# Layer 2's queries, keys, values and output projection by seven block products on the attention side

## The chip, the core and the metric

The kernel runs on one core of a Trainium2 chip. The metric is device time in microseconds (us) of that core, from launch to end; lower is better. The engines named below are PE (TensorE, matrix products), DVE (VectorE), ACT (ScalarE), POOL (GpSimd) and SP (SyncE, which here only issues DMA transfers). PEld is the loading of stationary operands into PE, and PEclk the clock that PE was granted, in parts of full speed.

## The reference

Four batches of 512 tokens by 512 features, in fp32, go through four layers. The layer that the change touches is layer 2, first half:

```
...
def _ln(x): ...                       # mean 0, variance 1 over features, eps 1e-6
qkv = (xin @ Wqkv.T + qkv_bias).reshape(Bs, Lx, 3, H, D)      # H = 16 heads of D = 32
sm  = exp(minimum(scale_mul_log, log(100)))
qn  = q / maximum(norm(q, axis=-1), 1e-12) * sm
kn  = k / maximum(norm(k, axis=-1), 1e-12)
p   = softmax(einsum('bhqd,bhkd->bhqk', qn, kn) + attn_bias)
o   = einsum('bhqk,bhkd->bhqd', p, v)  ->  (Bs, Lx, Cx)
attn = o @ Wproj.T + bproj
...
x = x + attn(_ln(x) * (scale1 + 1.0) + shift1) * gamma1
x = x + (gelu(( _ln(x) * (scale2 + 1.0) + shift2) @ Wfc1.T + bfc1) @ Wfc2.T + bfc2) * gamma2
```

Layer 0 is an attention with a sparse mask, layer 1 a full attention followed by a gated MLP, and layer 3 eight small experts with a 512 by 512 output. Layer 2 therefore has four products of 512x512 weights with 512x512 activations per batch ahead of its MLP: queries (`q2`), keys (`k2`), values (`v2`) and output (`proj2`).

## The kernel before

**Stages and streams.** Each batch passes through the stages `a01` (layers 0 and 1, attention), `m1` (layer 1's MLP), `a2` (layer 2's attention) and `m2` (layer 2's MLP, then the experts). Two streams of stages share the one core: stream A, the attention side, runs `a01`(1), `a2`(0), `a01`(2), `a2`(1), `a01`(3), `a2`(2), `a2`(3), and at the end the last batch's MLP `mlp2` and half of its experts; stream M, the other side, runs `a01`(0), `m1`(0), `m1`(1), `m2`(0), `m1`(2), `m2`(1), `m1`(3), `m2`(2) and the other half. `a2`(b) needs `m1`(b), and `m2`(b) needs `a2`(b).

**Who sets the order.** The kernel is written as generators that yield between products. A planner (`Clocks`, `interleave`) keeps an estimate of when every tile is written, how long each engine is held, and when each bank of PSUM is free; it lets the stream that is ready and furthest behind (by `WORK`, a length for each stage) take its next step. The planned start times then fix the order of instructions on each engine. On the chip an engine takes its own instructions in that order, each one waiting for its operands. In the planner, POOL's instructions and DVE's two-input ones between SBUF tiles also reserve a common `PORT` (`needs`). Side work (`chores`), such as forming sums of weights, runs in the same planner.

**Products.** `by_token` is the plain form: for each of four groups of 128 tokens, four products of 128x128 with 512 columns are summed in one PSUM bank. In `a2` all four projections had this form: 16 products of 512 columns each. `seven` is Strassen's scheme in the variant with few sums: weights and activations are cut into quarters of 256x256, the quarters and three sums on either side make seven block products, and each block product is four products of 128x128 with 256 columns, so 28 of 256 columns instead of 16 of 512. A `seven` works through parts 0 to 6; between them, part 0's result is copied out to a tile `u`, part 1's is added to it, part 3's goes with it into a tile `t`, and `take` receives the four quarters of the result, three of them with a tile still to be added:

```
x = yield from part(0);  u = side.u();  out(u, x)
y = yield from part(1);  free(y);       plus(u, y, u)
yield from part(2, x);   free(x);       take(0, 0, x, None)
y = yield from part(3);  t = side.t2(); plus(t, y, u)
x = yield from part(4);                 take(1, 1, x, t)
yield from part(5, y);   free(y);       take(0, 1, y, u)
yield from part(6, x);   free(x);       take(1, 0, x, u)
```

Before the change only side M used it, in `m1` and `mlp2_by_sevens`. The sums of activations are formed by `sums` on DVE or POOL (`add` takes the engine that the planner expects to end sooner).

**Weights.** Side M's weights come as a row of blocks (`Blocks`, tag `wm`, six tiles of two 128x512 blocks): four quarters and four sums, in the order of use; the sums are formed once by the chore `formed`, kept in DRAM, and reloaded for later batches. Side A had whole units (`Ring`, tag `wa`, two tiles of 128x4x512), loaded by one transfer of 1 MB each.

**Normalization.** After each group of 128 tokens of `q2` or `k2`, ACT squares the result (`t`), DVE sums each head's 32 squares (`ss`), POOL raises it to the power -0.5 (`inv`), for the queries DVE multiplies by `mul`, and DVE scales `t`; PE then transposes it (`heads_T`, tile `t`, L492) one product later. For `proj2`, the bias is added, POOL multiplies by the gate and adds into `x`.

In the profile, matrix products carry the line L486 and transposes L492; all DVE, ACT and POOL work carries L433, DMA loads L499.

## Time and profile before

| | |
|---|---|
| median of three runs | 2351.36 us (2350.81 to 2352.14) |
| the profiled execution's own time | 2346.66 us |
| its span, first to last instruction | 2344.9 us |
| mean granted PE clock | 0.995 |
| PE busy | 2284.7 us (97%) |
| DVE busy | 1423.9 us (61%) |
| ACT busy | 909.8 us (39%) |
| POOL busy | 876.6 us (37%) |
| DMA moved | 216.38 MB, queue of SP 28.6% of 16 engines |

An fp32 product appears in the records as two PE instructions, so a group that says x384 holds 192 products. Busy time of a group is time in which an instruction of it was the one in work; the mean of one also holds the tail in which the next is already running. The place of `a2`'s projections in the span can be read from the tile names: `q2`, `k2` and `v2` from 530 to 589 us for batch 0, 1045 to 1141 for batch 1, 1612 to 1706 for batch 2 and 1940 to 2000 for batch 3.

### The profile page before, as it was taken

How to read it: one execution, taken by the hardware profiler on the slowest of the kernel's cores; microseconds unless marked ns; L12 is line 12 of the kernel's file. 1: busy time of each engine (PE TensorE's matmuls, PEld its weight loads, DVE VectorE, ACT ScalarE, POOL GpSimd, SP SyncE). 2: the span in 40 equal slices, each digit the busy share in tenths (PEclk: the TensorE clock that was granted, in tenths of full speed). 3: DMA queues.
4: the chain of work that ended last, by engine and by line, in shares of the span. 5: the costliest groups of instructions: out<-in, count | busy, mean ns of one | idle time of the engine just before them, and what ended most of it. 6: DMA issues, size and time to landing. Idle time of an engine off the chain costs nothing.

```text
span 2344.9 us, 38165 instructions
## 1 busy us (share of the span) xinstructions
PE 2284.7 (97%) x14280; PEld 1582.9 (68%) x14280; DVE 1423.9 (61%) x3299; ACT 909.8 (39%) x2208; POOL 876.6 (37%) x1021
## 2 busy tenths in 40 slices
PE   8999999999999999999999999999999999999998
PEld 5655667885777777764677677775577786776444
DVE  5666676674675566756576465564576564785233
ACT  3665441012552452524454154243255313661313
POOL 5643321223343433433343352342334344454121
PEclk9999999999999999999999999999999999999999
DMA  3111223552224223231423323222322343223120
GB/s 117 37 60 55 83 89 115 182 184 81 73 73 122 68 100 121 77 113 36 133 80 95 117 82 104 90 77 77 99 78 86 109 148 97 75 73 126 51 82 25
DMA packets 137671, 216.38 MB, mean 92 GB/s; under 512 B 9792, under 2 KB 73312, under 8 KB 137488
## 3 DMA queue, kind: packets, MB, share of 16 engines
q1 hardware_dynamic: 136880, 213.72, 28.6%
q8 instruction: 114, 1.87, 0.3%
q14 instruction: 69, 0.57, 0.1%
q0 software_dynamic: 176, 0.15, 0.1%
q10 hardware_dynamic: 432, 0.07, 0.0%
HBM read 188.72 MB, written 25.18 MB: 91 GB/s over the span
## 4 chain that ended last, share of the span: by engine, by line
PE 54%; DVE 2%; ACT 1%; issue 1%; DMA 0%; POOL 0%; POOLq 0%; ACTq 0%; DVEq 0%
PE bank L486 39%; PE two L486 9%; PE bank L492 6%; ACT probs L433 1%; DVE mx L433 0%; PE two L492 0%; DVE probs L433 0%; DMA x<-in_x 0%; DVE hx L433 0%; DVE mt L433 0%; ACT pT L433 0%; ACT t L433 0%; DVE pT L433 0%; DVE t L433 0%; DMA arow<-in_rows 0%
## 5 line engine op out<-in xcount | busy, mean ns | idle before, releaser
L433 POOL TENSOR_SCALAR probs<-probs,inv 128x512 f32<-128x512 f32 (+4 forms) x544 | 328.1, 620 | 539.9 <-DVE inv L433 483.7
L433 ACT ACTIVATE probs<-probs,neg 128x512 f32<-128x512 f32 (+2 forms) x448 | 265.9, 595 | 188.1 <-DVE neg L433 182.9
L492 PEld LDWEIGHTS bank<-ident,probs 128*128 128x128 f32 (+1 forms) x1744 | 202.1, 141 | 82.3 <-issue 40.0
L492 PE MATMUL bank<-ident,probs 128*128 128x128 f32 (+1 forms) x1744 | 243.7, 275 | 5.1 <-ACT pT L433 3.7
L433 DVE CUSTOM_DVE_ANT_0 probs<-two,late 128x512 f32<-128x512 f32 x256 | 166.9, 685 | 34.8 <-PE two L486 23.7
L433 ACT COPY pT<-bank 128x512 f32<-128x512 f32 (+3 forms) x289 | 152.2, 547 | 68.2 <-PE bank L492 54.8
L486 PE MATMUL two<-kT,nq 32*128 32x512 f32 (+5 forms) x1088 | 149.1, 529 | 2.3 <-DVE neg L433 1.5
L433 POOL TENSOR_TENSOR inv<-ss,neg_half 128x16 f32<-128x16 f32 x32 | 92.9, 2902 | 124.4 <-DVE ss L433 124.4
L486 PE MATMUL bank<-wa_q,h 128*128 128x512 f32 x288 | 135.5, 594 | 0.3 <-ACT nq L433 0.3
L486 PE MATMUL bank<-pT,v 128*32 128x128 f32 (+2 forms) x3488 | 132.1, 275 | 3.4 <-DVE pT L433 2.1
L486 PEld LDWEIGHTS bank<-pT,v 128*32 128x32 f32 (+2 forms) x3488 | 113.2, 116 | 30.8 <-issue 17.3
L486 PE MATMUL bank<-mT,wm_gate 128*128 128x256 f32 x504 | 124.6, 382 | 3.3 <-DVE mp L433 1.5
L433 DVE COPY pT<-bank 128x512 f32<-128x512 f32 (+3 forms) x186 | 116.4, 635 | 7.2 <-PE bank L492 6.8
L433 POOL TENSOR_TENSOR x<-x,mt 128x512 f32<-128x512 f32 x60 | 80.3, 1342 | 100.4 <-DVE mt L433 100.4
L486 PEld LDWEIGHTS bank<-mT,wm_gate 128*128 128x128 f32 x504 | 92.7, 190 | 34.7 <-issue 17.5
L433 ACT COPY mu<-bank 128x512 f32<-128x512 f32 x41 | 23.9, 583 | 212.0 <-POOL x L433 108.1
L433 DVE TENSOR_REDUCE mx<-two 128x2 f32<-128x1024 f32 x64 | 77.8, 1216 | 45.2 <-PE two L486 45.1
L486 PE MATMUL bank<-wm_down,hid 128*128 128x256 f32 x408 | 101.5, 383 | 1.5 <-ACT mu L433 1.4
L433 DVE TENSOR_TENSOR x<-x,bank 128x512 f32<-128x512 f32 x93 | 63.4, 682 | 58.5 <-PE bank L486 57.9
L433 DVE RECIPROCAL inv<-total 128x2 f32<-128x2 f32 (+1 forms) x256 | 43.1, 168 | 89.5 <-ACT probs L433 76.5
L486 PE MATMUL bank<-wa_o,h 128*128 128x512 f32 x192 | 91.5, 594 | 0.0
L486 PE MATMUL bank<-mT,wm_up 128*128 128x256 f32 x360 | 89.3, 380 | 0.8 <-ACT mu L433 0.8
(389 smaller groups left out, 4694.9 us busy)
## 6 DMA issues: line engine op xcount, KB each, us to landing
wm_fc<-in_units SPq DMA_DIRECT2D x80, 256.0 KB, 2.9
wm_gate<-in_units SPq DMA_DIRECT2D x60, 256.0 KB, 3.0
wm_down<-in_units SPq DMA_DIRECT2D x52, 256.0 KB, 3.1
wm_up<-in_units SPq DMA_DIRECT2D x44, 256.0 KB, 3.0
wa_q<-in_units SPq DMA_DIRECT2D x10, 1024.0 KB, 5.2
wm_fc<-kept SPq DMA_DIRECT2D x32, 256.0 KB, 2.7
wm_fc<-kept SPq DMA_DIRECT2D x16, 512.0 KB, 3.3
wa_fc<-in_units SPq DMA_DIRECT2D x8, 1024.0 KB, 5.2
```

Source lines behind the costliest of these rows:

```text
L433: return call(*map(real, args), **{k: real(x) for k, x in kw.items()})
L486: latest[0] = nc.tensor.matmul(real(out), lhsT=real(lhsT), rhs=real(rhs), **kw)
L492: latest[0] = nc.tensor.transpose(real(out), real(src), unit)
```

## The change

`a2`'s four projections use `seven` on side A. The ring of side A becomes a row of blocks too (four tiles of two blocks, the same bytes), with a release for each block or unit; stages that take whole units take four blocks. The sums of `q2`'s and `k2`'s weights are formed by a new chore after 150 us of planned time, in tiles of side M that are free then, those of `v2` and `proj2` after `a01`(1) ends, in `pT` tiles; all are kept in DRAM and loaded from there by every batch. Activations are laid out in blocks, with `sums` for `hT` and `ctxT`. The normalization works on quarters (256 tokens by 256 features, as one 128x512 tile), in four tiles that rotate, and the transposes may lag by up to three quarters (`turns`). `proj2`'s bias times gate is added to `x` by a chore (`lift_x`) during the attention, and the result goes through `gated`. In the planner, POOL's power no longer reserves `PORT`, `scorable` and the experts' wait look at both double banks, and `a2`'s length becomes 120.8.

```diff
-WORK = {"a01": 157.8, "a2": 126.7, ...
+WORK = {"a01": 157.8, "a2": 120.8, ...
+LATER = 1.5
-WM = 6
+WM, WA = 6, 4
...
-    def needs(self, engine, op, outs, ins):
+    def needs(self, engine, op, outs, ins, func=None):
...
-        return (engine, "PORT") if wide and self.fast(outs + ins) else (engine,)
+        return (engine, "PORT") if wide and func != "pow" and self.fast(outs + ins) else (engine,)
...
-    ringA = Ring(load, clocks.tile, work, a["units"], "wa", 2, units_of(STREAM_A, ("a01", "a2", "mlp2", "half1")))
+    ringA = blocks("wa", WA, units_of(STREAM_A, ("a01", "a2", "mlp2", "half1")), A2_UNITS, False)
...
+    def formed_apart(names, staged):
+        for name in names:
+            a11, a12, a21, a22 = staged()
+            for x, which in ((a21, (1, 0)), (a22, (1, 1)), (a11, (0, 0)), (a12, (0, 1))):
+                load(quarters(x), ringA.source(name, which))
+            yield Until(lambda: clocks.written(a11, a12, a21, a22) + LATER)
+            add(a22, a21, a22, ALU.add)
+            add(a21, a11, a21, ALU.subtract)
+            add(a11, a22, a11, ALU.subtract)
+            add(a12, a12, a11, ALU.subtract)
...
+                    sync.dma_start(out=kept[:, j - at.start, :], in_=x)
+            ringA.formed.add(name)
+
+    def formed_for_a2():
+        yield Until(150.0)
+        yield from formed_apart(A2_UNITS[:2], lambda: [*sideM.sums(), sideM.u()])
+        yield When(lambda: ("a01", 1) in ended)
+        yield from formed_apart(A2_UNITS[2:], lambda: halved(sideA.pT(2)))
...
         def scorable():
-            return max(locked[0], clocks.free("two", 2, 2))
+            return max(locked[0], clocks.free("two", 2), clocks.free("two", 2, 2))
...
-        yield from turned(side, n, hT, b, coefs["s1"], coefs["h1"])
-        qT, late = side.n(), None
+        yield from turned(side, n, hT, b, coefs["s1"], coefs["h1"], blocks=True)
+        *extra, own = halved(side.pT(2))
+        right, turn = sums(hT, extra), halved(side.pT(2))
+        qT, late = side.n(), []
...
-                ps = yield from by_token(side, t, hT, unit)
...
+        def turns(leave=0):
+            while late and (len(late) > leave or clocks.written(late[0][3]) <= clocks.now):
+                dst, i, j, q = late.pop(0)
...
+        def normed(dst, bias, by):
+            def put(i, j, bank, more):
+                q, sq = turn[0], side.t2()
+                turn.append(turn.pop(0))
...
+                late.append((dst, i, j, q))
+                return turns(3)
...
+        yield from seven(side, "q2", right, False, normed(qT, qb, mul), u=own)
+        yield from seven(side, "k2", right, False, normed(kT, None, None), u=own)
+        yield from seven(side, "v2", right, False, valued, u=own)
+        pb, gate = side.row(a["rows"][R_PROJ : R_PROJ + 1, :]), side.row(gates[0, b : b + 1, :])
+        lifted = lift_x(b, pb, gate)
...
-        def finish(t, ps):
-            u = side.t1()
-            vector.tensor_tensor(u, ps, pb, ALU.add)
-            gpsimd.tensor_tensor(u, u, gate, ALU.mult)
-            gpsimd.tensor_tensor(xs[b][:, t, :], xs[b][:, t, :], u, ALU.add)
-
-        yield from project_out(side, ctxT, side.ring.take("proj2"), finish)
+        *extra, own = (qT[:, i, :] for i in range(4))
+        yield When(lambda: len(lifted) == NT)
+        yield from seven(side, "proj2", sums(ctxT, extra), False, gated(side, b, gate), u=own)
```

## The prediction

> **What bounds the kernel now.** I read the page first, for the share of each engine and the granted clock. Then the groups by line, for the two forms of product.

> ```profile
> span 2344.9 us, 38165 instructions
> PE 2284.7 (97%) x14280; PEld 1582.9 (68%) x14280; DVE 1423.9 (61%) x3299; ACT 909.8 (39%) x2208; POOL 876.6 (37%) x1021
> L486 PE MATMUL bank<-wa_q,h 128*128 128x512 f32 x288 | 135.5, 594 | 0.3 <-ACT nq L433 0.3
> L486 PE MATMUL bank<-mT,wm_gate 128*128 128x256 f32 x504 | 124.6, 382 | 3.3 <-DVE mp L433 1.5 <-ACT mu L433 1.3 <-ACT mT L433 0.4
> L486 PEld LDWEIGHTS bank<-mT,wm_gate 128*128 128x128 f32 x504 | 92.7, 190 | 34.7 <-issue 17.5 <-DVE mp L433 1.9 <-ACT mu L433 1.7
> ```

> PE is at work for 97% of the span; only 2344.9 - 2284.7 = 60.2 us are idle. So PE's own work sets the time, and the question is what one product of either form costs when products follow each other. The means (594 and 382 ns) can't say, since they hold each instruction's tail. The timeline of PE where the two streams alternate does, by its start times.

> ```profile
> 1284.42 1.02 PE L486 MATMUL bank<-wa_proj,h 128*128 128x512 f32 x2
> 1285.28 1.03 PE L486 MATMUL bank<-wm_up,hid 128*128 128x256 f32 x4
> 1286.14 0.59 PE L486 MATMUL bank<-wa_proj,h 128*128 128x512 f32 x1
> ```

> Two instructions (one product of 512 columns) hold PE from 1284.42 to 1285.28, 0.86 us; four instructions (two products of 256) from 1285.28 to 1286.14, again 0.86 us. A product of half the columns costs half, 0.43 us. Third, busy time in stretches (length, then PE, PEld, DVE, ACT, POOL, each with its number of instructions): side M alone with sevens, and the queries, keys and values of batches 0 and 1.

> ```profile
> 392.00:522.00 130.00, 123.40 (x579) 107.29 (x578) 90.72 (x146) 14.46 (x24) 33.56 (x26) 1.00 0.57 186
> 530.00:589.00 59.00, 59.00 (x196) 34.09 (x195) 26.33 (x49) 14.36 (x24) 23.20 (x8) 1.00 0.23 76
> 1045.00:1141.00 96.00, 91.49 (x334) 46.79 (x333) 49.06 (x102) 32.65 (x54) 34.93 (x17) 1.00 0.29 95
> ```

> Plain products starve PE of nothing in batch 0; in batch 1, 4.5 us are lost. One side's sevens with no other stream lose 130 - 123.40 = 6.6 us. Last, what ended those waits: the waits of PE in 1045 to 1141, then two of the four that the timeline shows in 392 to 522.

> ```profile
> PE bank L492 <- DVE t L433: 4.3, 2, 2.7
> 445.12 1.99 PE L486 MATMUL bank<-mn,wm_up 128*128 128x256 f32 x8 [1.78 <-DVE mt L433]
> 504.25 1.97 PE L486 MATMUL bank<-wm_down,hx 128*128 128x256 f32 x8 [1.92 <-DVE hx L433]
> ```

> The first is the transpose that waits for a normalized `t`. The second is a seven whose product came late because four sums of `wm_down` (441.72 to 444.4, 0.69 us each) stood ahead of it in DVE's queue.

> **The change part by part.** The order of instructions in the changed kernel has 256 products of 512 columns fewer (16 projections of 16) and 448 of 256 columns more (16 of 28); the transposes are the same in number, and 13 products on `ident` that only filled idle time at the start are gone.

> 1. Products: -256 x 0.86 + 448 x 0.43 = -220.2 + 192.6 = **-27.5 us**, all on the engine that sets the end. This needs the weight loads to stay covered: one takes 190 ns and an instruction of 256 columns holds PE for 215 ns, so 25 ns of cover are left; the timeline row above has them covered. [...]

> 2. Waits for a normalized `t`: 4.3 us in batch 1 and 2.7 us in batch 2 (1612 to 1706), 0 in batches 0 and 3. Transposes may now lag by three quarters, so most of this goes; late next is the last quarter of the keys, which is still waited for ahead of the scores. **-5 us**, bounds -7.0 and 0.

> 3. Waits within the 16 new sevens. No row shows two sides' sevens next to each other. The nearest is side M alone: 579 instructions less 24 small ones are 9.9 sevens of 56, and 6.6/9.9 = 0.67 us each. 16 x 0.67 = **+10.7 us**. Bounds: 0, if the other stream always fills in, and the longest of those waits, 1.92 us, in every seven, +30.7 us.

> 4. Sums of weights and activations, and the other DVE and POOL work. DVE has 114 instructions more, POOL 6 more; 16 sums of weights are formed once. At 0.69 us (the `wm_down` sums) DVE's 114 are 79 us, 1424 to about 1503 of 2325 us, 65%: no bound. Where they lie matters: those of `v2` and `proj2` (two groups of four) come after `a01`(1) ends, in the very stretch where side M is alone, and there a group of four on DVE made PE wait 1.78 us. **+2 us**, bounds 0 and 8 x 0.69 = 5.5. Those of `q2` and `k2` lie around 150 to 250 us, where two streams run and DVE is at 29 us of 50; I cost them at nothing, and without that cover at another 5.5 us.

> 5. POOL's power no longer reserves the port in the planner, so DVE's scaling of `t` may be planned beside it. The timeline has two such overlaps: the scaling at 1087.95 took 0.71 us under a power that began at 1087.90, the median of 32 is 0.692. [...] **0**; if POOL held DVE for a whole power, 32 x 2.9 = 93 us would be at stake, of which these rows show nothing.

> 6. DMA. Three more blocks of 256 KB for each of 16 units, 4 units loaded and their sums stored once: 12.6 + 4.2 + 4.2 = 21 MB on 216, and SP issues 132 transfers more, at 0.37 us 49 us on a queue that does nothing else. The stores of sums wait on SP for DVE, and side M's loads stand behind them; its ring is six tiles deep and a load lands in 2.9 us. In the list of what PE waited for there is no transfer of weights. **0**; uncovered, one landing per unit, 16 x 2.9 = 46 us.

> 7. `proj2`'s bias and gate move ahead into the attention: five additions a batch for POOL (37% busy) or DVE, where POOL's `x` additions take 1.3 us each and nothing but the last product waits for them. The quarters' three gate multiplications and additions per batch replace as many as go. **0**.

> Sum: -27.5 - 5 + 10.7 + 2 = **-19.8 us**. The profiled execution took 2346.66 us, so it would take 2326.9; the median of the runs, 2351.36, stands 4.7 us above it, and I carry the difference over: 2351.36 - 19.8 = **2331.6 us**. With all good ends (-34.5) it is 2316.9, with all bad ones (+8.7) 2360.1. The start adds noise of either sign that I don't cost: at 50 to 65 us and 105 to 115 us the granted clock fell below 1, which cost some 7 us, and a new order may have more or fewer such falls.

> **The rivals.** (a) Slower: DVE's queue hands the sevens' results on too late. A seven has four places where PE needs a result of DVE or ACT within one or two products (the copy of part 0, two additions, the freed bank), 64 in all. The gain of 30.5 us ahead of this term is gone at 0.48 us a place, and the kernel is over 0.2% slower from 0.55 us. Price: at every second place the mean of the four waits of M alone (1.78, 1.34, 1.51, 1.92: 1.64 us) is +52 us, so 2373. For it: the queries' norms are DVE work of 0.68 + 0.17 + 0.18 + 0.69 us a quarter, the additions of the quarter come on top, and the plain products that could always run are gone; of 59 us in batch 0 DVE was busy 26, and with some 14 us more in 54 us it is at 74%. Against it: side M alone had DVE at 90.7 of 130 us, 70%, and lost 0.17 us a place; in three of four batches another stream is there.

> (b) No change: weights come late now and then, for the ring holds only eight blocks, 14 us of products. One landing of 2.9 us at every second unit is 8 x 2.9 = 23 us, which leaves +3. Against it: side M lives from such a ring without a wait for it.

> (c) Over 32 us gained: side M fills all gaps, the waits for `t` go, and the better planned port saves more. That the change does not do what it says can be excluded: the order has the 448 products.

> **How the numbers follow.** A measurement of this kernel can tell about 0.2%, 4.7 us. The forecast, 5 to 32 us gained, has 0.74; (a) 0.14; (b), within 4.7 us, 0.07; (c) 0.05. The two gaining cases give 0.79 faster, (b) 0.07 the same, (a) 0.14 slower. The range goes from 2319 (-32) to 2351, which takes the forecast and the better half of (b), and leaves out (a), (c) and the rest of (b), some 0.2.

> **What would show it.** Right: PE busy about 2257 us, the groups of `wa_q`, `wa_k`, `wa_v`, `wa_proj` with 256 columns at 0.86 us for four instructions, PE idle 60 to 75 us, waits on DVE `t` in the transposes shorter. Wrong: idle of PE above 90 us, ended by DVE `pT` or `nq` within side A's sevens (a), by transfers of `wa` (b), or instructions of 256 columns more than 216 ns apart when both sides run sevens.

## The result, and the profile after

The changed kernel takes 2367.61 us (median of 4 runs, 2365.03 to 2368.99); the kernel before took 2351.09 us beside it. The ratio is 1.0072, with a 95% interval of 1.0055 to 1.0090: slower by 17 us, where 20 us of gain were forecast. The profiled execution took 2365.03 us, its span is 2363.1 us, 18.2 us more than before. Everything below is told against these spans, or as a ratio to runs of the kernel before on the same chip; 0.001 of ratio is 2.35 us.

The page of the changed kernel, span and PE (busy time, share of the span, instructions):

```profile
span 2363.1 us, 39362 instructions
...
PE 2271.8 (96%) x14638; PEld 1663.7 (70%) x14638; DVE 1503.6 (64%) x3413; ACT 919.6 (39%) x2218; POOL 892.3 (38%) x1027
```

PE has fewer columns to do, and its busy time fell, but only by 12.9 us instead of 27.5. Its idle time rose from 60.2 to 2363.1 - 2271.8 = 91.3 us. So two things ate the gain: 31.1 us of new waits, and 14.6 us that are missing from the fall of busy time. The products themselves are not the reason. The timeline of PE in batch 3, where the sevens of the values run on side A:

```profile
1979.46 1.89 PE L493 MATMUL bank<-wa_v,pT 128*128 128x256 f32 x8
1981.19 1.89 PE L493 MATMUL bank<-wa_v,h 128*128 128x256 f32 x8
1982.91 0.60 PE L499 MATMUL two<-ident,pT 128*128 128x128 f32 x4
```

Eight instructions of 256 columns hold PE from 1981.19 to 1982.91, 0.215 us each, as before. What is missing is clock. The mean granted clock fell from 0.995 to 0.988. Between the warm-up and the last 30 us the clock rows show 12 stretches of half clock, ten of 3.41 us and two of 6.83, where the kernel before has two, one of 10.24 and one of 3.41 us; each stretch of 3.41 us does the work of 1.7 us: in these stretches instructions of 256 columns begin 0.427 us apart (median of 46 in the changed kernel), elsewhere 0.216. The last experiment below agrees: at the old clock of 0.995 the same products keep PE busy for 2256.7 us, and 2284.7 - 27.5 is 2257.2.

Where the waits are is read from busy time in stretches (length, then PE, PEld, DVE, ACT, POOL with their instructions, clock, DMA share, GB/s). After: side M alone, the queries, keys and values of batch 0 and of batch 1, and the attention of batches 1 and 3; then two lines of before, side M alone and the attention of batch 3.

```profile
392.00:535.00 143.00, 130.80 (x607) 112.43 (x606) 99.31 (x161) 16.66 (x27) 40.62 (x31) 0.99 0.62 202
535.50:577.00 41.50, 41.50 (x209) 36.61 (x209) 29.07 (x54) 13.28 (x23) 23.89 (x9) 1.00 0.39 128
...
1050.00:1138.00 88.00, 84.98 (x393) 59.48 (x392) 54.78 (x108) 31.83 (x54) 35.81 (x18) 0.98 0.32 105
1138.00:1317.00 179.00, 174.51 (x1388) 138.44 (x1387) 120.57 (x279) 84.87 (x195) 70.25 (x83) 0.98 0.32 106
...
1991.00:2143.00 152.00, 145.99 (x1263) 114.60 (x1262) 108.20 (x260) 90.12 (x190) 71.55 (x85) 0.99 0.26 83
```

```profile
392.00:529.00 137.00, 129.84 (x615) 112.57 (x614) 97.27 (x157) 17.20 (x28) 34.88 (x27) 1.00 0.56 181
...
1999.40:2137.30 137.90, 137.72 (x1210) 102.65 (x1209) 105.15 (x253) 79.85 (x181) 71.41 (x85) 1.00 0.26 81
```

The sevens' own products wait for nothing: none of their 896 instructions on `wa` has 0.1 us of idle time before it, and PE is busy for 41.50 of 41.50 us in batch 0, with DVE at 70%. The 3.0 us in batches 1 and 2 are a transpose's. Length less PE gives the idle time of each stretch:

| stretch | idle before, us | after, us |
|---|---|---|
| start, to 392 | 20.0 | 24.9 |
| side M alone | 7.2 | 12.2 |
| queries, keys, values, batches 0 to 3 | 0, 4.5, 3.0, 0 | 0, 3.0, 3.0, 0 |
| attention of layer 2, batches 0 to 3 | 1.85, 0.8, 0.8, 0.2 | 2.7, 4.5, 4.2, 6.0 |
| layers 0 and 1 of the next batch beside mlp2 | 7.0, 4.5 | 9.7, 6.6 |

The waits of PE, summed by what ended them, show a new head of the list (before, `neg` had 3.0 us and the transposes waited 7.4 us for `t`):

```profile
PE two L493 <- DVE neg L440: 11.2, 8, 2.9
PE two L499 <- DVE mt L440: 6.0, 2, 3.0
PE bank L499 <- DVE pT L440: 5.8, 6, 2.0
PE bank L493 <- DVE mp L440: 4.7, 3, 2.3
```

`neg` is the row minimum from which softmax starts (the CUSTOM_DVE lines below), and PE's next scores wait for the bank that it reads. One such wait in full, in the timeline of all engines:

```profile
792.44 0.33 SPq L506 DMA_DIRECT2D mrow<-gates  x1
...
795.77 0.69 DVE L440 TENSOR_TENSOR mrow<-mrow,mrow 128x512 f32<-128x512 f32 x1 [0.46 <-DMA mrow<-gates]
...
796.54 1.26 POOL L440 TENSOR_TENSOR x<-x,mrow 128x512 f32<-128x512 f32 x1 [5.33 <-DVE mrow L440]
...
796.59 1.76 DVE L440 TENSOR_TENSOR x<-x,mrow 128x512 f32<-128x512 f32 x1
...
798.27 0.28 DVE L440 CUSTOM_DVE_ANT_0 probs<-two,mask 128x128 f32<-128x128 f32 x1
...
799.26 0.60 PE L493 MATMUL two<-kT,nq 32*128 32x195 f32 x4 [2.01 <-DVE neg L440]
```

`lift_x` has put the product of bias and gate on DVE, where it waits 0.46 us for the gate's load; then one of the additions into `x`, which takes 1.76 us on DVE, because POOL began the same kind of addition 0.05 us earlier (at 1719.24 us, with POOL idle, one takes 0.69). All minima but one stand behind both, and PE is idle for 2.01 us. It happens again at 1371 us; at 1714 and 1996 us, in the attention, the wait for the load is 2.19 and 1.60 us and PE idles 1.55 and 1.60 us. Before, `lift_x` did not exist: POOL did the products and the additions into `x`, waited for the gate itself, and no wait of PE ended with them.

### The profile page after: what moved, and what is told of

It is laid out like the page before. It is cut to its first block, busy times and chain, and to the rows that moved or that the text cites. A ratio compares the mean times of both kernels' runs of the same rounds, so it can differ in the third digit from the quotient of the medians.

```text
span 2363.1 us, 39362 instructions
## 1 busy us (share of the span) xinstructions
PE 2271.8 (96%) x14638; PEld 1663.7 (70%) x14638; DVE 1503.6 (64%) x3413; ACT 919.6 (39%) x2218; POOL 892.3 (38%) x1027
## 3 DMA queue, kind: packets, MB, share of 16 engines
q8 instruction: 117, 1.92, 0.3%
## 4 chain that ended last, share of the span: by engine, by line
PE 68%; DVE 5%; ACT 3%; issue 3%; DMA 2%; POOL 1%; POOLq 0%; DVEq 0%; ACTq 0%; SPq 0%
PE bank L493 49%; PE two L493 11%; PE bank L499 8%; ACT probs L440 2%; DVE probs L440 1%; PE two L499 1%; DMA arow<-gates 1%; DMA mrow<-gates 0%; POOL probs L440 0%; DVE x L440 0%; DVE st L440 0%; DVE hx L440 0%; ACT pT L440 0%; DVE hid L440 0%; DMA x<-in_x 0%
## 5 line engine op out<-in xcount | busy, mean ns | idle before, releaser
L440 ACT COPY pT<-bank 128x512 f32<-128x512 f32 (+3 forms) x303 | 160.5, 551 | 91.2 <-PE bank L499 68.0
L440 DVE CUSTOM_DVE_ANT_0 probs<-two,late 128x512 f32<-128x512 f32 x256 | 166.7, 685 | 30.0 <-PE two L493 18.2
L493 PE MATMUL bank<-wa_q,h 128*128 128x512 f32 (+1 forms) x272 | 102.4, 506 | 0.3 <-ACT nq L440 0.3
L440 POOL TENSOR_TENSOR x<-x,t 128x512 f32<-128x512 f32 x32 | 40.5, 1266 | 146.7 <-DVE t L440 146.4
```

The costliest lines, as they stand in the source:

```text
L440: return call(*map(real, args), **{k: real(x) for k, x in kw.items()})
L493: latest[0] = nc.tensor.matmul(real(out), lhsT=real(lhsT), rhs=real(rhs), **kw)
```

## The experiments

Two theories to begin with. **Theory 1**: the loss is made in DVE's queue outside the sevens, by `lift_x` and by the weight sums of `v2` and `proj2` in side M's stretch alone, and the longer waits are followed by half clock. **Theory 2**: the edits of the planner (the port, the banks) made a worse order, or any new order is off by some 10 us.

**The lift on POOL.**

```diff
-            add(row, row, gate, ALU.mult)
+            gpsimd.tensor_tensor(row, row, gate, ALU.mult)
...
-                add(xs[b][:, t, :], xs[b][:, t, :], row)
+                gpsimd.tensor_tensor(xs[b][:, t, :], xs[b][:, t, :], row, ALU.add)
```

> The changed kernel with the bias times gate and its additions into x (lift_x, used by layer 2's attention and by its MLP on side M) always on POOL instead of whichever of DVE and POOL the planner picks. Theory 1, the loss comes from work in DVE's queue outside the sevens, lift_x first: the waits of PE at about 797, 1370, 1714 and 1996 us (2.0 + 2.3 + 1.6 + 1.6 = 7.5 us) and the falls of the clock that follow them (17 us at half, so 8.5 us) go; about 2352 us. Theory 2, the planner's other edits or the mere re-planning cost the time: no less than 2362 us.

Measured: ratio 0.9999 (0.9986 to 1.0013), 2354.31 us. The whole loss is gone: 0.0073, 17 us. In the trace POOL waits 4.74 us for the same gate, and the gaps behind DVE near 797, 1371, 1714 and 1996 us are no longer there.

```profile
798.06 1.27 POOL L440 TENSOR_TENSOR mrow<-mrow,mrow 128x512 f32<-128x512 f32 x1 [4.74 <-DMA mrow<-gates]
799.41 1.26 POOL L440 TENSOR_TENSOR x<-x,mrow 128x512 f32<-128x512 f32 x1
```

The four gaps (2.01, 2.30, 1.55, 1.60) sum to only 7.5 us. PE's busy time fell by 8.6 us too, to 2263.2, with the same instructions. Most of that is half clock: behind the four gaps the changed kernel has five windows of 3.41 us at half clock, 8.5 us lost, and here one is left. The rest is falls that came and went elsewhere; up to 582 us the order on PE is the same in both kernels, yet batch 0's queries start 3.4 us later in this execution.

POOL is not free of the same trouble. In batch 2's attention its product waits for the gate with the scaling of `probs` behind it, PE waits 2.27 us for that, and this is where the one window at half clock is left:

```profile
1705.77 1.27 POOL L440 TENSOR_TENSOR arow<-arow,arow 128x512 f32<-128x512 f32 x1 [18.37 <-DMA arow<-gates]
...
1708.20 1.63 PE L499 MATMUL bank<-ident,probs 128*128 128x128 f32 x8 [2.27 <-POOL probs L440]
```

**The sums early.** All four units' sums are formed at 150 us, where two streams run.

```diff
-        yield from formed_apart(A2_UNITS[:2], lambda: [*sideM.sums(), sideM.u()])
-        yield When(lambda: ("a01", 1) in ended)
-        yield from formed_apart(A2_UNITS[2:], lambda: halved(sideA.pT(2)))
+        yield from formed_apart(A2_UNITS, lambda: [*sideM.sums(), sideM.u()])
```

> The changed kernel with the weight sums of v2 and proj2 formed early too, together with those of q2 and k2 after 150 us in side M's tiles, and not in the stretch where side M is alone. Theory 1: PE's idle time between 390 us and the start of batch 0's queries falls from 12.2 to about 7 us and the fall of the clock at 443 us goes, so the queries start some 6 us earlier; about 2361 us. Theory 2: no such gain at the end, within 4 us of 2367.6 either way.

Measured: 1.0049 (1.0032 to 1.0066), 2364.08 us; 5 us better than the changed kernel, whose interval it overlaps (1.0055 to 1.0090). Side M's stretch alone is again 137 us long with 137 - 130.39 = 6.6 us idle:

```profile
392.00:529.00 137.00, 130.39 (x614) 112.53 (x613) 98.32 (x157) 16.61 (x27) 35.90 (x28) 1.00 0.56 183
```

**The port of the power, as before.**

```diff
-        return (engine, "PORT") if wide and func != "pow" and self.fast(outs + ins) else (engine,)
+        return (engine, "PORT") if wide and self.fast(outs + ins) else (engine,)
```

> The changed kernel with one planner edit undone: POOL's power reserves the common port again. Theory 1: this edit is not the cause, 2364 to 2371 us. Theory 2, the edit lets the planner promise DVE time that the chip does not give: back to about 2352 us.

Measured: 1.0022 (1.0009 to 1.0034), 2358.42 us. Neither value: 12 us better than the changed kernel, far more than theory 1 allowed for. In the trace its idle time is 5.8 us less, most of it in the start, whose order this edit changes too: at 108 us PE waits 2.60 us for `t` as in the kernel before, in the changed kernel 3.29 us. But batch 0's queries start no sooner for it (535.7 against 535.3 us), since the start has more half clock. The span is shorter only behind batch 2's queries, by 8.8 us: 1.4 us of it are idle time, and 10.2 us run at half clock there instead of 25.9. The waits of 3.02 us for `mt` and of 2.28 us for `mp` at the end of the last attention are gone in this order, although the gaps at 799 and 1371 us stay (2.27 and 2.21 us). Why this order avoids those waits stays open.

**The three edits of the planner in the kernel before.**

```diff
+        return (engine, "PORT") if wide and func != "pow" and self.fast(outs + ins) else (engine,)
...
+            return max(locked[0], clocks.free("two", 2), clocks.free("two", 2, 2))
...
```

> The kernel before with the three planner edits of the change alone (the power without the port, scorable and the experts' wait looking at both double banks). Theory 1: within 4 us of the kernel before, 2347 to 2355 us. Theory 2: the edits carry the loss, 2360 us or more.

Measured: 0.9992 (0.9981 to 1.0002), 2351.49 us. By themselves these edits cost nothing that the times show, although PE waits 3.29 us at 105 us here too. That removes the first half of theory 2, except for the 12 us above, which only show with the rest of the change.

**Another plan of the changed kernel.** `MARGIN = 0.4` instead of 0.3.

> A control: the changed kernel with the planner's margin 0.4 instead of 0.3, nothing else; the order of the instructions changes in many places. Theory 1: the same structure has the same waits, 2366 us within 4. Theory 2 (the loss is an accident of this plan): off by more than 6 us, to either side.

Measured: 1.0077 (1.0059 to 1.0095), 2369.83 us, against 1.0072. The order is different in many places, yet gaps of 1.4 to 2.9 us stand near 796, 1142, 1371, 1713 and 1995 us again. In this plan the loss is the same, and so are its places. That speaks against the second half of theory 2, though the 12 us of the planner's edit show that an order can matter that much. The changed kernel itself was not run again beside the experiments; this near copy, and the bank alone below with 1.0066, stand for it on other chips.

**Lift and sums together.** Both edits from above.

> The changed kernel with both edits: the bias and gate of proj2 and of mlp2 lifted into x on POOL alone, and the sums of all four weight units formed at 150 us. Theory 1 (DVE's queue outside the sevens, each long wait followed by half clock): the two gains add, 12 us of the lift and 3 of the sums, so about 2351 us (2347 to 2354), with no gap of PE over 1.5 us at 797, 1370, 1714 and 1996 us nor falls of the clock there or at 443 us. Theory 2 (any new plan moves the time by some 10 us either way): the gains need not add, anything from 2345 to 2366.

Measured: 0.9979 (0.9967 to 0.9991), 2349.93 us. The ratio is 0.0093 or 22 us under the changed kernel, the sum of 17 and 5 (20 by the repeat below). The two costs are separate, and together they are all of the loss and 3 to 5 us of gain.

**Only queries, keys and values by sevens.** The output projection in rows as before (side A's row of blocks, the layout of `ctxT` and `a2`'s length, 122.3, follow):

```diff
-        lifted = lift_x(b, pb, gate)
...
-        yield from seven(side, "proj2", sums(ctxT, extra), False, gated(side, b, gate), u=own)
+        yield from project_out(side, ctxT, unit, finish)
```

> Part of the change: queries, keys and values by sevens, the output projection plain as before (its bias and gate after it, in rows), its sums of weights not formed. Theory 1: the gain in products is three quarters (20.6 us instead of 27.5), the two lifts of the attention go (half of the lift's 12 us, 6), and four of eight sums in side M's stretch alone go (1.5 us): 2366 + 6.9 - 6 - 1.5 = about 2365 us. Rival (the output's seven itself, with its sums of activations and its hand-over to mlp2, is what loses): 2352 or below. Rival (the sevens of queries, keys and values lose it all): 2372.

Measured: 1.0026 (1.0013 to 1.0039), 2359.83 us, 5 us under the 2365 of theory 1 and over the 2352 of its rival. The lifts of mlp2 are still in it, and its gaps at 792 and 1370 us are 2.45 and 2.28 us. So `proj2`'s part is neither the whole loss nor free of it.

**The lift planned 6 us later.**

```diff
+            yield Until(lambda: clocks.written(row, gate) + 6.0)
             add(row, row, gate, ALU.mult)
```

> The changed kernel, the lift free to go to DVE or POOL, but its first step is planned 6 us later than the row and the gate are expected, so that the load of the gate has landed when DVE comes to it. If the wait for the gate's load at the head of DVE's queue is what costs: as much as with POOL alone, about 2354 us. If it is DVE's work on the lift (additions of 1.76 us beside the same on POOL) ahead of the softmax's minimum: a third of that gain, about 2362 us.

Measured: 1.0031 (1.0020 to 1.0043), 2360.75 us, 10 us better. The trace says why it is half way: in the attention the planner now gives all four products to POOL, so the edit did more than delay them, and DVE no longer waits for the gate; in mlp2 the order on DVE stayed as it was (gaps of 2.35 and 2.02 us).

**Product or additions.** One kernel has only the product on POOL, the other only the additions.

> The changed kernel; of the lift only the product of row and gate is put on POOL, the additions into x stay free to go to DVE (nine of them do in the plan). If what costs is that DVE waits at the head of its queue for the load of the gate: the whole gain of the lift on POOL, about 2354 us. If it is an addition of 1.76 us on DVE beside the same on POOL: 2362 us or more.

> The mirror: the product of row and gate free (on DVE in the plan), all additions into x on POOL. If the wait for the gate's load costs: 2362 us or more. If the additions on DVE cost: about 2354 us. If either alone is enough to keep the softmax's minimum late, both this and the other are near 2360.

Measured: 1.0024 (1.0013 to 1.0034) and 1.0029 (1.0015 to 1.0044), 2358.67 and 2359.10 us: the third case, either edit alone brings 10 to 11 of the 17 us. The traces tell which is which. With the product alone on DVE (first two lines, additions on POOL), DVE still waits 0.43 us for the gate in mlp2, but no addition stands ahead of the minima and PE waits 0.30 instead of 2.01 us. With the additions alone free to go to DVE (last two lines), the addition begins 0.05 us ahead of POOL's and takes 0.69 us, while POOL's takes 1.78; PE waits 1.04 us.

```profile
795.63 0.69 DVE L440 TENSOR_TENSOR mrow<-mrow,mrow 128x512 f32<-128x512 f32 x1 [0.43 <-DMA mrow<-gates]
...
797.45 0.60 PE L493 MATMUL two<-kT,nq 32*128 32x195 f32 x4 [0.30 <-ACT probs L440]
```

```profile
796.22 0.69 DVE L440 TENSOR_TENSOR x<-x,mrow 128x512 f32<-128x512 f32 x1 [0.16 <-POOL mrow L440]
...
797.34 0.60 PE L493 MATMUL two<-kT,nq 32*128 32x195 f32 x4 [1.04 <-DVE neg L440]
```

In mlp2 it is the addition, in the attention the wait for the gate: with the product on DVE, gaps of 1.32 and 1.30 us stay at 1708 and 1990 us. With the product on POOL these two go, and PE waits 2.11 us for `probs` at 1709 us instead, as with the whole lift on POOL.

**The lift's cost put into the kernel before.**

```diff
-        gpsimd.tensor_tensor(fb, fb, gate, ALU.mult)
-        for t in range(NT):
+        vector.tensor_tensor(fb, fb, gate, ALU.mult)
+        vector.tensor_tensor(xs[b][:, 0, :], xs[b][:, 0, :], fb, ALU.add)
+        for t in range(1, NT):
             gpsimd.tensor_tensor(xs[b][:, t, :], xs[b][:, t, :], fb, ALU.add)
```

> The kernel before with one suspected cost put in: in mlp2 of batches 0 to 2 the product of bias and gate and the first of the four additions into x are DVE's instead of POOL's; nothing else of the change. Theory 1 (DVE's queue is held by the load of the gate and by an addition that runs beside POOL's, ahead of the softmax's minimum): PE idle for about 2 us at two or three places that had none, each followed by 3.4 us at half clock, so 2353 + 2 to 3 x (2 + 1.7) = 2360 to 2364 us. If the lift on DVE costs only where sevens of the attention side are about: 2353.

Measured: 1.0016 (1.0001 to 1.0031), 2354.88 us: 4 us in the ratio, none in the trace, whose span of 2345.3 us is that of before; no gap came. A miss for theory 1 as it was put. The timeline shows two differences: the gate's load was issued at 786.94 us, 5.7 us ahead of the product (in the changed kernel 3.3 us; two loads of `wa_q` from 785.79 us on stood ahead of it on SP), so DVE does not wait; and the addition comes at 821 us, not ahead of the minima.

```profile
792.64 0.68 DVE L433 TENSOR_TENSOR mrow<-mrow,mrow 128x512 f32<-128x512 f32 x1
793.65 0.29 DVE L433 CUSTOM_DVE_ANT_0 probs<-two,mask 128x128 f32<-128x128 f32 x1 [0.32 <-PE two L486]
...
821.26 0.68 DVE L433 TENSOR_TENSOR x<-x,mrow 128x512 f32<-128x512 f32 x1
```

So the lift on DVE is not dear in itself. In the runs here it is dear where the order puts it ahead of the minima with a load that is not there yet, or with POOL already at the same work.

**What makes the clock fall.** In the clock rows of the changed kernel's trace all 14 falls (the twelve and two in the last 30 us) begin at multiples of 3.4133 us from each other, to 0.005 us. What brings one is asked in a kernel of its own: products of 512 columns, and between them waits of PE for DVE in nine settings, each eight times:

```diff
+    for g in range(72):
+        ...
+        nc.vector.tensor_scalar(t[:, 0:wide], p[:, 0:wide], 0.001, None, ALU.mult)
+        for _ in range(more):
+            nc.vector.tensor_scalar(t, t, 0.5, None, ALU.mult)
+        p = run(40 + shift, t)
```

> A stream of products of 512 columns, 17 to 20 us long, 72 times, and between them waits of PE for a chain of one to five DVE operations; the rest of the computation is left out, the output is no result. If a fall of the clock is decided by the idle time within one window of a fixed grid of 3.413 us (half of it or more): falls of 3.413 us start on one grid after gaps of about 2 us only where the gap lies within one window, and gaps of over 3.4 us always bring one. If it is decided by the length of the gap alone: one length divides those with a fall from those without.

Measured: ten falls between the first product and the last, all of 3.413 us, all starting at multiples of 3.413 us from each other. The waits of 1.57 and 1.80 us (16) were never followed by one. Of the eight of 2.17 us four were, of the eight of 2.63 us six. Two of the waits of 2.17 us, each as two windows of that grid, the one with the wait and the next (columns as above, but no ACT):

```profile
704.63:708.04 3.41, 1.24 (x4) 0.33 (x3) 1.97 (x4) 0.00 (x0) 0.99 0.00 0
708.04:711.46 3.42, 3.42 (x5) 1.36 (x6) 0.43 (x1) 0.00 (x0) 0.51 0.00 0
2479.56:2482.97 3.41, 1.79 (x5) 0.48 (x3) 1.51 (x3) 0.00 (x0) 1.00 0.00 0
2482.97:2486.39 3.42, 2.87 (x7) 1.44 (x8) 0.89 (x3) 0.00 (x0) 1.00 0.00 0
```

The first wait lies in one window (1.24 of 3.41 us busy, 2.17 idle) and the next window runs at half clock. The second, just as long, is cut by the grid into 1.62 and 0.55 us, and nothing follows. In all 32 waits of over 1.5 us the larger part decides: up to 1.80 us no fall, from 2.01 us on always one. So a wait of 2 us costs 2 us or 3.7 us, by where it happens to lie. A wait of over 3.4 us, which the expectation names too, does not occur in this kernel. Half of a window, 1.71 us, is too low a bound for this kernel, since 1.80 us brought no fall; 2.01 us were enough. In the full kernels the bound is less sharp: in the changed one a window with 1.34 us idle (from 22.9 us) is followed by a fall, one with 1.74 us (from 425.7 us) is not. And there two of the twelve falls last two windows, such as the one behind the wait of 1.55 us at 1714 us, which therefore costs 5 us.

**Statistics of `x` later.** With the lift on POOL and the sums early a gap of 2.9 us is left near 1136 us, behind DVE's wait for a load of `x`.

```diff
+        if b == 3:
+            yield Until(lambda: clocks.written(xs[b]) + 4.0)
         yield from norm_steps(n, xs[b], 1e-5)
```

> The changed kernel with the lift on POOL and the sums early (2349.9 us), and also the first statistics of x of batch 3 planned 4 us later, so that DVE does not wait for the load of x at the head of its queue. If that wait makes the gap of PE of 2.9 us near 1136 us: the gap and the fall of the clock behind it go, 2.9 + 1.7 = 4.6 us less, about 2345 us. If the softmax there is late for another reason: 2350.

Measured: 0.9988 (0.9978 to 0.9998), 2349.97 us, the gap is still there. The planner expects that load so much too early that the edit moved no instruction: this is a second measurement of lift and sums together (0.9979), and tells how well a ratio repeats, 0.0009.

**A bank of side A for the transposes**, on top of it, and alone in the changed kernel.

```diff
-                yield Until(side.at, of=[q])
-                p = side.bank()
+                yield Until(lambda: side.own() if side.own() < math.inf else side.at(), of=[q])
+                p = side.own_bank() if side.own() < math.inf else side.bank()
```

> As e11_x_late, and the transposes of the normalized quarters take a bank of side A rather than one of the shared pair of banks. If the waits of 3.02 us near 1092 and 1656 us (which took the place of the two of 2.75 us for a normalized row) come from the shared bank that an expert's result still holds: up to 6 us less than e11_x_late. If DVE is late there whatever bank is used, or the two banks of side A are wanted by the sevens: the same as e11_x_late or slower by up to 5.

> The changed kernel with nothing but the bank: transposes of the normalized quarters take a bank of side A, not one of the shared pairs. With the lift on POOL and the sums early the same edit brought 11 us. If that was the two waits of 3.02 us and what follows them: 6 to 11 us here too, about 2358 us. If it was an accident of where the waits fell on the clock's windows: 2362 to 2370.

Measured: 0.9943 (0.9928 to 0.9957), 2338.86 us, on top of the other two edits; 1.0066 (1.0051 to 1.0082), 2368.92 us, alone. The waits of 3.02 us of the transposes become 2.49 us of an expert's product that waits for DVE in the same place:

```profile
1100.59 0.66 PE L499 MATMUL two<-ident,pT 128*128 128x128 f32 x4 [3.02 <-DVE mt L440]
```

```profile
1118.62 1.23 PE L493 MATMUL bank<-wm_out,hid 128*128 128x512 f32 x2 [2.48 <-DVE mT L440]
```

(The first line is of the changed kernel, the second of the one with the bank alone.) DVE is late there, whatever bank is used, and alone the edit gains 0.0006, less than a repeat differs. The 11 us on top of the other two edits are not explained by it. In the profiles the span fell by 11.4 us, 5.9 of them in the first 392 us, where PE's order is the same in both kernels and only the clock's windows fall otherwise; that part is the run's, not the edit's. The other 5.5 us lie behind the last batch's queries, where the wait of 2.27 us for `mp` at 2132 us and the half clock behind it are gone. But the median times of 11 and 5 runs differ by 11 us too. Why the new order earns that stays open, as with the planner's edit above.

**The load of `x` told later**, on top of the lift on POOL, the sums early and the bank. The planner is told that the load of batch 3 lands 8 us later.

```diff
+        if b == 3:
+            xs[b].tile.marks[:] = [(lo, hi, t + 8.0 if wrote else t, wrote) for lo, hi, t, wrote in xs[b].tile.marks]
```

> The best so far (lift on POOL, sums early, own bank: 2338.9 us), and the planner told that the load of x of batch 3 lands 8 us later, which moves its statistics behind four pieces of the softmax (e11_x_late had moved no instruction). If DVE's wait for that load makes the gap of 3.95 us at 1135 us: that gap and the fall behind it go, 4 to 5.5 us less, about 2334 us. If the softmax is late there anyway: 2339.

Measured: 0.9933 (0.9916 to 0.9950), 2337.24 us. The gap of 3.95 us and the fall behind it are gone. Without and with the edit (DVE and PE, then DVE):

```profile
1134.36 2.47 DVE L440 BATCH_NORM_STATS2 st<-x 128x6 f32<-128x512 f32 x4 [2.81 <-DMA x<-in_x]
...
1138.65 1.57 PE L493 MATMUL two<-kT,nq 32*128 32x512 f32 x4 [3.95 <-DVE neg L440]
```

```profile
1130.23 0.69 DVE L440 CUSTOM_DVE_ANT_0 probs<-two,late 128x512 f32<-128x512 f32 x1
...
1131.37 0.67 DVE L440 CUSTOM_DVE_ANT_0 probs<-two,late 128x512 f32<-128x512 f32 x1
```

The profiled span fell by 5.6 us, the ratio by 0.0010, which is within what a repeat gives. This version is faster than both kernels, by 0.7% and 1.4%. Its page:

```profile
span 2331.2 us, 39343 instructions
...
PE 2256.7 (97%) x14638; PEld 1652.2 (71%) x14638; DVE 1487.2 (64%) x3395; ACT 915.5 (39%) x2215; POOL 913.4 (39%) x1046
```

With a mean clock of 0.995, that of the kernel before, PE's busy time is 28.0 us under it. The idle time is 74.5 us, 14.3 more than before; the largest parts are 5.6 us in the start and two waits of 1.85 us in the last attention.

## Why the prediction was wrong, step by step

**Step 7 failed, and it is the case.** It cost the lift of bias and gate at nothing, because POOL has room and "nothing but the last product waits for them". Both are beside the point. The prediction asked who waits for the lift, not who stands behind it: `add` gives each operation to the engine that the planner thinks soonest, that was DVE for six of seven products and ten of 28 additions, and behind them in DVE's queue stood the minima, for which PE waits at once. Nor did it count that the change puts mlp2's bias and gate, until then on POOL, through the same helper; two of the four gaps lie there. The gate's load that the same step moves was not followed through SP's queue either. The lift on POOL takes 17 us off, though POOL's queue makes one such wait in its turn.

**The clock was not costed after the start.** The prediction set falls aside as noise of the start. Of the 18.2 us of span that were lost, PE's busy time shows 14.6 as half clock: -27.5 + 31.1 + 14.6 = 18.2. The price behind a wait of 2 us, 1.7 us and in two places 3.4, stands in no row of waits; only the clock in the rows of the stretches shows it, 0.98 in batch 1's rows above.

**Step 4 had the right place and less than half the size**: +2 forecast, 5 measured by forming the sums early, inside its bounds of 0 and 5.5. Idle time rose by 5.0 us in side M's stretch.

**Step 3 was too dear**: +10.7 for waits within the sevens, and 0 measured. Side M alone was the nearest row, and it was the wrong one: in batch 0, where only 12 of 209 instructions are side M's, PE was busy for 41.50 of 41.50 us, and the other 13 sevens had no wait either.

**Step 2 was mis-sized**: -5 forecast. Waits of 4.3 and 2.7 us for `t` went, and 3.02 us each for `mt` came in the same two places: -1. The prediction had looked for what is late next in the keys; it was an expert's result in DVE's queue, for which the transpose's bank was held. Two such results (1.53 us from 1086.21 us) lay on DVE in the old wait too, but POOL's power ended no sooner there (2.90 us from 1084.81 us), so which of them made it is not shown.

**Step 1 held** to half a microsecond: 2257.2 us of PE forecast at the old clock, 2256.7 in the last experiment. An instruction of 256 columns holds PE for 0.215 us here, half of the 0.43 of one of 512 in the prediction's rows. **Step 6 held** as far as weights go; the list of PE's waits has no transfer of `wa`. **Step 5** said 0 for the power. As a price on the engines that held: in the changed kernel 16 scalings overlap a power and take 0.68 to 0.73 us, with a median of 0.692 over all 32. But undoing the planner's edit gains 12 us in this kernel, by the order that it makes; why is not settled.

**The rivals.** (a) named the right engine in the wrong place: DVE handed results on too late, not those of the sevens but those of the softmax beside and after them. Its sign came true without its mechanism. (b) did not happen. What the prediction wrote down as wrong, idle time above 90 us, came (91.3), but ended first by `neg`, outside side A's sevens, and by `mt`, at two of their transposes. The largest waits for `pT` (2.02 and 1.92 us) are for copies of transposed probabilities in the last attention.

Where the attention of batches 1 to 3 loses 3 to 6 us each is shown only in part: the lift, and the load of `x` in batch 1. The waits of 1.85 us in the last attention stay in the best version. Their timeline shows a reciprocal on DVE that waits 2.82 us for ACT's exponentials while ACT loads tables (1.28 us each) between Gelu and exponential; that this comes from another phase between the two sides was not tried.

## What to carry to other kernels

Cost a step that is moved by what stands behind it in its engine's in-order queue, not by who reads its result: an operation that waits for a load there is a wait for everybody behind it. Where a helper chooses the engine by itself, put such a step on the engine whose queue holds least that the bound engine needs next; here that was POOL, and one wait of 2.27 us behind it remained. And when TensorE is the bound, price a wait of 2 us at up to 3.7, with the 1.7 us lost at half clock behind it, and at more where the fall lasts two windows (5 us for a wait of 1.55 here): look for the half-clock window behind it before calling a wait small.

## What the runs showed of the hardware

Of two additions of 128x512 in SBUF, one on DVE and one on POOL, the one that started first kept its time here and the other was held up: DVE's took 0.69 us alone (1719.24 us) and 1.76 us when POOL's began 0.05 us earlier (796.59 us); where DVE's began 0.05 us earlier, it took 0.69 us and POOL's 1.78 instead of 1.26 (796.22 us, product on POOL), and in the changed kernel 0.69 us and 1.77 (1917.90 us). The prediction weighed an overlap for POOL's power, where 16 overlaps cost DVE at most 0.04 us, and not for the lift, where it costs over 1 us.
